# The first layer's hand-written list of steps in another order

## The chip, the cores and the metric

The kernel runs on one core of a Trainium2 chip. The time is that of one execution on the device, in microseconds (us), from start to end; the median of three runs is given. A core has five engines that run side by side, each through its own queue and in order: TensorE (PE, matrix products; its weight loads are shown as PEld), VectorE (DVE), ScalarE (ACT), GpSimd (POOL) and SyncE (SP, here a queue for transfers). They wait for each other by semaphores.

## The reference

A graph network of three layers over 2500 nodes with 256 features and 80000 edges sorted by destination. Cut to what matters:

```python
def _edge_conv(x, src, dst, W, b):
    xi = x[dst]; xj = x[src]
    m = jnp.concatenate([xi, xj - xi], axis=-1) @ W + b
    s = jax.ops.segment_sum(m, dst, num_segments=N)
    cnt = jax.ops.segment_sum(jnp.ones((dst.shape[0],), m.dtype), dst, num_segments=N)
    return s / jnp.maximum(cnt, 1.0)[:, None]

h = jnp.maximum(_layernorm(x, axis=-1), 0.0)
xs = [h]
for W, b in ((W0, b0), (W1, b1), (W2, b2)):
    h = jax.nn.relu(_edge_conv(h, src, dst, W, b)); xs.append(h)
out = x + jnp.concatenate(xs, axis=-1) @ Wf + bf
```

## The kernel before

**Tiles.** The nodes are 20 tiles of 128, taken in ten pairs q = 0 to 9. The sum over the edges is a product with a matrix of counts, `a`: how many edges go from node m to node n. It is built on the chip from the list of edges and used by all three layers. A window is six destinations; 417 windows stand in five groups of up to 84, and a step of counting takes four windows at a time (b = 0 to 104; 0 to 20 are the first group).

**Staging.** Layer 0 has two hand-written lists of step names, `order` (line 906) and `later` (line 1151). The program goes through both, one name after the other, and each name issues its instructions (table `acts`, from line 889, and `steps`, from line 1141). An engine keeps the order in which its instructions were issued; across engines only data and free buffers count. So the list sets the order within each engine's queue and nothing else. Layers 1 and 2 and the end follow by loops that the change leaves alone.

**The steps of `order`, by what they do** (the number behind a name is the pair, the part of the edges, or the counting step):

- Start: `dstr` (ACT) copies the destinations; `lim`, `first`, `pi` (`find_rows`, DVE), `next`, `pk` (`pick_half`, PE), `sg` (`count_half`, ACT), `se` (`search`, DVE), `pb` (PE) and `sa` (DVE) search where each of four parts of the edges begins. `io` (`small_numbers`, ACT) makes three small tables. `ge` (`get_edges`, POOL) gathers the edges of a part by two indirect DMAs.
- Layer norm: `st` (`stats`, DVE, a pair of tiles), `sq` (ACT), `sc` and `of` (DVE), for the groups of pairs 0, 1, 2 to 3, 4 to 7 and 8 to 9. Then the pair's two tiles are normalized: `N` on POOL twice, `Nd` on DVE twice, `Nm` on DVE and ACT, `Np` on POOL and ACT (`normalize`, line 751).
- Products: `T` (`turn`, PE) turns a pair, `R` (`take_turned`, ACT) copies it out, `Z` and `F` (`product`, PE) multiply it by the layer's and the last weights; `H` (ACT) and `L` (DVE) split Z's result in a high and a low part, `V` (DVE) adds a bias, `G` (ACT) takes F's.
- Keys of a part of the edges: `aw` (ACT); `kr` (`find_room`), `kw`, `ka` (`key_parts`), `kb` (`key_high`) and `kc` (`key_node`) on DVE; `km` (ACT); `kt` (`key_turn`, PE); `k1` and `k2` (`key_copy`, ACT). In the profile these write `room`, `away`, `lo_i`, `es` or `hi_i`, `kn`, `km`, and `key_m` and `key_n`.
- Counting: `B` (`compare`, line 825, DVE) compares keys with a row of numbers, for two counting steps at once, by one instruction for `one_m` and two for `one_n`; a `B` whose step was done already does nothing. `C` (`counts`, PE) multiplies them; `E` (`take_counts`, ACT) copies the counts to `a`.
- `warm` stores how many matmuls without use the next product, turn or pick on PE issues first:

```python
def keep_warm(n):
    cold[0] = n
```

**Buffers.** `one_m` and `one_n` have three buffers each (`AT_ONCE`), and two PSUM banks of one pool serve `pk`, `pb`, `kt` and `C` up to the first `g`.

**The steps of `later`:** `g` begins a group's sum, `u` is one tile of it (four matmuls), `o` its own term, `r` its end; `c` is a turn of up to four counting steps for the next group on PE, `e` takes one, `b` compares two; `d` finds degrees; `f` writes a finished group to memory; `x` adds the input by a DMA on POOL's queue; the rest prepare weights and the next layer.

**Loads.** The transfers of the input and the first weights are issued ahead of both lists (lines 414 to 457): x in five chunks, `own_w` (the second half of the layer's weights, needed by `Z`), the last weights (needed by `F`), and the first half.

Of the kernel before, what the change touches and what calls it, by code (L numbers as in the profile page):

```python
# [298 lines left out]
def by_windows(ctx: ExitStack, tc: tile.TileContext, x, src, dst, Ws, bs, Wf, bf, out, missing):  # L299
# [130 lines left out]
    ws = [None] * L  # L430
# [88 lines left out]
    first = pp.tile([P, 1], F32, name="first")  # L519
# [358 lines left out]
    def by_count(g):  # L878
# [25 lines left out]
        "warm": keep_warm,  # L904
    }
    order = """
        warm7 dstr lim first st0 sq0 io next pi0 sc0 of0 Nm0 pi1 st1 pk00 sg00 se00 st2 warm4 pk01 sg01 se02 T0
        R0 sq1 sc1 se01 of1 pk10 pk30 se04 se03 sg30 sg10 Z0 st4 pk20 Np1 pk21 sg21 T1 st5 st6 F0 sg20 pk11 st7
        se10 ge0 R1 st3 pb0 sa0 G0 sq3 sc3 F1 st9 aw0 kr0 ka0 H0 se11 kb0 sg11 pk31 kw0 Nd7 sg31 Z1 N6 T6 se12
        kc0 se14 km0 sq2 sc2 G1 T7 se13 st8 R6 ge1 kt0 k10 pb1 of3 sa1 sq4 Nm5 sc4 R7 L0 k20 of4 Nm9 H1 Z6 F6 T9  # L910
        B0 B1 aw1 kr1 T5 G6 of2 F7 R5 R9 C0 ge2 aw2 G7 C1 E0 E1 Z9 Np8 B2 B3 B5 V9 C2 E2 C3 T8 H6 B4 kw1 ka1 kb1
        ge3 Z5 L1 kc1 E3 C5 km1 kr2 aw3 H5 ka2 kb2 kr3 L5 kt1 k11 kw3 k21 ka3 N2 T2 R2 kw2 Z7 C6 kb3 C4 kc2 Z2
        E5 R8 B7 kc3 C7 B6 Nm3 km3 C8 E4 km2 T3 E6 N4 T4 kt2 L6 E7 E8 B9 H9 L9 kt3 k13 Z8 C10 k22 k23 k12 C9 R3
        Z3 H2 B8 B11 B12 H7 L7 E10 E9 C12 E12 B13 C11 E11 L2 H3 F3 G3 C14 E14 C13 F5 B10 B15 C16 C15 R4 Z4 B17
        E13 E15 E16 C17 C18 G5 F4 B19 C19 H8 L8 E17 E18 H4 C20 F2 G4 E20 E19 B16 B18
        """

    second = ctx.enter_context(ExitStack())
# [56 lines left out]
    E12 = 4096.0  # L975
    C1 = 1.0 + 1.0 / E12
# [160 lines left out]
    def take_next(it=iter(range(len([b for b in windows if b[0] == 0]), len(windows)))):  # L1137
# [11 lines left out]
        "h": each((late_final, (q,)) for q in LATE),  # L1149
    }  # L1150
    later = """
        g d u u d u u L3 B23 ws w B21 d d u u c B24 B14 G2 L4 d d e B22 B20 u u u e e e b b b c e d u e e d d d
        f u u b b u c u b u e e d y u e e x b c o o o e e e b c e x b b b e e e u o e u e d d c e u u r d d g u
        w u u b w c e u d e e d d d b u b w u u e c b e e e e u f u c u e u u x u u b b b e e c e d d d u u y p
        e e o e e o b c u p o e b d d e d e u u e d d c b b b e u d y p o r g u u c e e u u b b u u u u d e e c
        e o o b u y e e e c b b e e u u e u e u c p o u u u e o b b c b b b u e e e f u u e e d e e c p e u r g
        u u c e d d u f b b u u u u c u u d e e e u o e e b b c b o e e e e e b p u u u u c e e b b d b b u e e
        u b c u e u u k e e e d d e c e y o s u o r f s s v g v v u u u s u u u u u p v q u l u o u u u q o u u
        u u u n n n p o n l q q h h o u u r x
        """  # L1160
    acts.update(steps)
    for name in (order + later).split():
# [269 lines left out]
    for l in range(1, L):  # L1432
# [7 lines left out]
        for i in range(Q + LAG):  # L1440
            if 0 < i <= Q:
                lone.make(i - 1)
            if i < Q:
                q = order[i]
                n = Nodes(l, q)
# [53 lines left out]
    for i, q in enumerate(order):  # L1499
# [9 lines left out]
        for k in range(2):  # L1509
            t = 2 * q + k  # L1510
            add_to_acc(t, po[k])
            n = P if t < NT - 1 else LAST
            if i < Q - 4 and q < Q - 1:
                if k:
                    d = SPo.dma_start(out[(t - 1) * P:(t + 1) * P, :].rearrange("(k p) d -> p k d", p=P),
                                      acc[:, t - 1:t + 1, :])
            else:
                d = (ACTo if i >= Q - 4 and k else SPo).dma_start(out[t * P:t * P + n, :], acc[:n, t, :])
# [11 lines left out]
def gnn_kernel(tc: tile.TileContext, x, src, dst, Ws, bs, Wf, bf, out):  # L1530
    nc = tc.nc
    with tc.tile_pool(name="flag", bufs=1) as flag:
        missing = flag.tile([1, 1], I32, name="missing")
        tc.mark_branch_hint_location("again", "LikelyTaken",
                                     engines=[getattr(mybir.EngineType, e) for e in ("PE", "DVE", "Activation")])
        near_end = by_windows(tc, x, src, dst, Ws, bs, Wf, bf, out, missing)
        loads, (again,) = nc.values_load_multi_w_load_instructions(missing, min_val=0, max_val=1)

        for d in loads:
            if d.ins.engine in [getattr(mybir.EngineType, e) for e in ("PE", "DVE", "Activation")]:  # L1540
                tc.add_manual_dep(d.ins, near_end.ins.name,
                                  mybir.DependencyInfo(mybir.DependencyClass.Sync, mybir.DependencyReason.DATA),
                                  reason="behind the outputs")
        with tc.If(again > 0, label="again"):
            general(tc, x, src, dst, Ws, bs, Wf, bf, out)
# [28 lines left out]
```

## Time and profile before

| | us |
|---|---|
| median of three runs | 460.54 (460.31 to 460.66) |
| the profiled execution | 459.55 |
| its span, from the first to the last instruction | 457.6 |

The profile is of one execution. Its page gives the busy time of each engine and, in 40 slices of 11.4 us, the busy share in tenths. A row of the timeline has the start (us from the span's start), the duration, the engine, the operation, what it writes and reads, and in brackets how long the engine had been idle before it and what ended that. Several equal instructions in a row are one row (x2). The durations of rows on one engine overlap a little, since an instruction begins before the one ahead has quite ended; so the distance from start to start is what it costs in a queue. A row of the windows has, after the stretch and its length, the busy us (and the instructions) of PE, PEld, DVE, ACT and POOL, then the granted clock of PE as a share of full speed, the share of the DMA engines and GB/s.

### The profile page before, as it was taken

The numbers are of one execution on the slowest core, as the hardware profiler recorded it, in microseconds if no ns is written. First come the engines' busy times: TensorE is split into PE (matmuls) and PEld (weight loads), VectorE is DVE, ScalarE is ACT, GpSimd is POOL, SyncE is SP. The second block draws the span as 40 slices with busy tenths as digits, with TensorE's granted clock in tenths as the row PEclk, the third lists the DMA queues.
The fourth block names the chain that finished last, engine by engine and source line by source line (L and its number), as shares of the span: only waits on it lengthen the run. The fifth ranks groups of instructions, "written<-read, shape, count | busy, mean of one in ns | idle before, by whom it ended". The sixth has DMA issues, their size and how long they took to land.

```text
span 457.6 us, 7441 instructions
## 1 busy us (share of the span) xinstructions
PE 447.6 (98%) x2733; PEld 358.2 (78%) x2733; DVE 375.2 (82%) x724; ACT 319.7 (70%) x586; POOL 41.2 (9%) x64
## 2 busy tenths in 40 slices
PE   6999999999999999999999999999999999999995
PEld 3887887788888878878878868867888787688685
DVE  7999989899998755299979859876999687569795
ACT  6888877785757553587879849756877897597540
POOL 4690103111001010100000000000000000000000
PEclk9999999999999999999999999999999999999999
DMA  8310179882629276341396522011124855220015
GB/s 279 101 47 1 24 149 151 171 136 51 122 58 183 51 184 141 98 93 45 115 362 227 181 91 92 0 45 47 46 56 146 319 185 178 90 92 1 1 62 166
DMA packets 22056, 52.47 MB, mean 115 GB/s; under 512 B 1931, under 2 KB 12382, under 8 KB 22014
## 3 DMA queue, kind: packets, MB, share of 16 engines
q1 hardware_dynamic: 14654, 33.83, 22.3%
q0 software_dynamic: 5856, 16.48, 18.9%
q10 hardware_dynamic: 1504, 1.63, 1.0%
q8 instruction: 22, 0.36, 0.3%
q14 instruction: 20, 0.16, 0.1%
HBM read 36.47 MB, written 15.62 MB: 114 GB/s over the span
## 4 chain that ended last, share of the span: by engine, by line
PE 92%; DVE 4%; DMA 2%; issue 0%; ACT 0%; SPq 0%
PE bank L267 92%; DMA own_w<-in_L_gnn_W_dram 2%; DVE one_m L267 1%; DVE one_n L267 1%; DVE acc L267 0%; DVE lo_i L267 0%; DVE room L267 0%; DVE st L267 0%; DVE zl L267 0%; SPq L267 0%; DVE away L267 0%; DVE kn L267 0%; DVE es L267 0%; ACT away L267 0%; ACT acc L267 0%
## 5 line engine op out<-in xcount | busy, mean ns | idle before, releaser
L267 ACT CAST block<-staged 128x1008 fp32r<-128x1008 bf16 x120 | 118.0, 1031 | 16.7 <-DVE staged L267 6.4
L267 PE MATMUL bank<-block,zh 128*128 128x504 f32 (+1 forms) x200 | 83.7, 418 | 0.0
L267 PE MATMUL bank<-a,zh 128*128 128x504 f32 (+1 forms) x200 | 80.3, 401 | 0.0
L267 PE MATMUL bank<-a,zl 128*128 128x504 f32 (+1 forms) x200 | 77.9, 389 | 0.0
L267 PE MATMUL bank<-block,zl 128*128 128x504 f32 (+1 forms) x200 | 77.2, 386 | 0.0
L267 ACT CAST a<-bank 128x480 fp32r<-128x480 f32 (+1 forms) x105 | 52.8, 566 | 25.3 <-PE bank L267 25.0
L267 PE MATMUL bank<-block,sh 128*128 128x504 f32 x160 | 69.1, 432 | 0.0
L267 DVE TENSOR_TENSOR one_m<-iota_m,key_m 128x2048 bf16<-128x2048 bf16 (+2 forms) x55 | 64.2, 1166 | 6.0 <-PE bank L267 6.0
L267 PE MATMUL bank<-block,sl 128*128 128x504 f32 x160 | 62.5, 390 | 0.0
L267 PE MATMUL bank<-block,staged 128*128 128x512 f32 (+1 forms) x288 | 62.4, 368 | 0.0
L267 PEld LDWEIGHTS bank<-block,staged 128*128 128x128 f32 x288 | 49.4, 188 | 9.9 <-issue 0.7
L267 DVE TENSOR_TENSOR block<-staged 128x1008 fp32r<-128x1008 bf16 x40 | 47.0, 1205 | 5.3 <-PE bank L267 3.9
L267 PEld LDWEIGHTS bank<-block,zh 128*128 128x128 f32 x200 | 37.6, 188 | 10.8 <-issue 2.3
L267 PEld LDWEIGHTS bank<-block,zl 128*128 128x128 f32 x200 | 37.6, 188 | 10.6 <-issue 3.2
L267 PEld LDWEIGHTS bank<-a,zl 128*128 128x128 f32 x200 | 37.7, 188 | 7.0 <-issue 0.2
L267 PEld LDWEIGHTS bank<-a,zh 128*128 128x128 f32 x200 | 37.6, 188 | 7.0 <-issue 0.2
L267 DVE TENSOR_TENSOR one_n<-iota_n,key_n 128x640 bf16<-128x640 bf16 (+2 forms) x110 | 42.5, 428 | 0.0
L267 PEld LDWEIGHTS bank<-block,sh 128*128 128x128 f32 x160 | 30.1, 188 | 10.5 <-issue 3.5
L267 PEld LDWEIGHTS bank<-block,sl 128*128 128x128 f32 x160 | 30.1, 188 | 9.3 <-issue 3.7
L267 DVE TENSOR_TENSOR staged<-staged 128x1008 bf16<-128x1008 bf16 x40 | 27.2, 679 | 12.0 <-ACT block L267 11.6
L267 PEld LDWEIGHTS <-one_m 128*128 128x128 bf16 x834 | 29.2, 98 | 9.0 <-issue 3.5
L267 PE MATMUL bank<-own_w,hT 128*128 128x256 f32 x144 | 34.8, 386 | 0.7 <-DMA own_w<-in_L_gnn_W_dram 0.7
(192 smaller groups left out, 641.7 us busy)
## 6 DMA issues: line engine op xcount, KB each, us to landing
staged<-a_dram SPq DMA_DIRECT2D x52, 504.0 KB
a_dram<-a POOLq DMA_DIRECT2D x20, 630.0 KB, 8.8
acc<-in_x_dram POOLq DMA_DIRECT2D x3, 640.0 KB, 8.8
out_dram<-acc SPq DMA_DIRECT2D x5, 256.0 KB
acc<-in_x_dram SPq DMA_DIRECT2D x2, 512.0 KB
acc<-in_x_dram ACTq DMA_DIRECT2D x1, 768.0 KB
out_dram<-acc SPq DMA_DIRECT2D x5, 128.0 KB
wt<-in_L_gnn_W_dram SPq DMA_DIRECT2D x2, 256.0 KB
```

Of the source, the lines that this page charges most:

```text
L267: return self.tc.keep_in_program_order(call(*args, **kwargs))
```

## The change

The two lists get another order. All names appear as often as before; nine names that stood in `later` (B14, B20 to B24, G2, L3 and L4) now stand in `order`'s text, ahead of the first `g`. No function changes.

```diff
--- before.py
+++ after.py
@@ -904,15 +904,16 @@
         "warm": keep_warm,
     }
     order = """
-        warm7 dstr lim first st0 sq0 io next pi0 sc0 of0 Nm0 pi1 st1 pk00 sg00 se00 st2 warm4 pk01 sg01 se02 T0
-        R0 sq1 sc1 se01 of1 pk10 pk30 se04 se03 sg30 sg10 Z0 st4 pk20 Np1 pk21 sg21 T1 st5 st6 F0 sg20 pk11 st7
-        se10 ge0 R1 st3 pb0 sa0 G0 sq3 sc3 F1 st9 aw0 kr0 ka0 H0 se11 kb0 sg11 pk31 kw0 Nd7 sg31 Z1 N6 T6 se12
-        kc0 se14 km0 sq2 sc2 G1 T7 se13 st8 R6 ge1 kt0 k10 pb1 of3 sa1 sq4 Nm5 sc4 R7 L0 k20 of4 Nm9 H1 Z6 F6 T9
-        B0 B1 aw1 kr1 T5 G6 of2 F7 R5 R9 C0 ge2 aw2 G7 C1 E0 E1 Z9 Np8 B2 B3 B5 V9 C2 E2 C3 T8 H6 B4 kw1 ka1 kb1
-        ge3 Z5 L1 kc1 E3 C5 km1 kr2 aw3 H5 ka2 kb2 kr3 L5 kt1 k11 kw3 k21 ka3 N2 T2 R2 kw2 Z7 C6 kb3 C4 kc2 Z2
-        E5 R8 B7 kc3 C7 B6 Nm3 km3 C8 E4 km2 T3 E6 N4 T4 kt2 L6 E7 E8 B9 H9 L9 kt3 k13 Z8 C10 k22 k23 k12 C9 R3
-        Z3 H2 B8 B11 B12 H7 L7 E10 E9 C12 E12 B13 C11 E11 L2 H3 F3 G3 C14 E14 C13 F5 B10 B15 C16 C15 R4 Z4 B17
-        E13 E15 E16 C17 C18 G5 F4 B19 C19 H8 L8 E17 E18 H4 C20 F2 G4 E20 E19 B16 B18
+        io dstr warm4 lim first st0 sq0 warm7 next pi0 pk00 sg00 sc0 pi1 of0 Nm0 pk01 sg01 st1 sq1 se00 T0 R0
+        pk10 st2 pk20 sg20 sg10 sc1 se02 se01 of1 se04 se03 Np1 ge0 Z0 H0 st5 st7 pk30 sg30 pb0 sa0 T1 R1 st6
+        st4 sq3 F0 se10 pk31 se11 sg31 sc3 aw0 st3 sq2 pk11 sg11 N6 F1 pk21 sg21 st9 G1 Z1 Nd7 se12 G0 se13 of3
+        se14 T6 kr0 ge1 R6 H1 st8 sq4 pb1 kw0 ka0 T7 R7 kb0 L0 sc2 F6 kc0 km0 kt0 sa1 k10 k20 sc4 of4 Nm9 F7 Nm5
+        ge3 B0 B1 T9 ge2 aw1 kr1 R9 T5 ka1 Np8 Z6 C0 N2 kb1 N4 kw1 R5 C1 G7 of2 H6 B2 B3 Z9 L6 V9 B5 B4 kc1 Nm3
+        E0 E1 T8 aw2 aw3 C3 R8 C2 Z5 E2 L1 T2 G6 C5 B7 B6 C4 E3 km1 kr2 R2 Z7 E5 H5 kr3 C6 E4 ka2 ka3 H9 kt1 k11
+        Z2 k21 kw3 kb3 km2 C7 kb2 E6 C8 kw2 L5 km3 kc3 kc2 T3 E7 E8 T4 R4 B9 kt3 k23 k13 kt2 k22 B8 Z8 k12 L9
+        C10 R3 C9 Z3 H7 B11 C12 H2 C11 F3 E10 E9 L7 E12 E11 B12 B13 B10 C14 C13 L2 H8 F5 E14 E13 B15 C15 C16 Z4
+        G3 G5 B17 B19 C18 C17 F4 L8 E15 E16 C20 B16 B18 H4 E17 H3 B23 B21 B24 L4 B14 E18 C19 F2 E20 E19 G4 B22
+        B20 L3 G2
         """
 
     second = ctx.enter_context(ExitStack())
@@ -1149,14 +1150,14 @@
         "h": each((late_final, (q,)) for q in LATE),
     }
     later = """
-        g d u u d u u L3 B23 ws w B21 d d u u c B24 B14 G2 L4 d d e B22 B20 u u u e e e b b b c e d u e e d d d
-        f u u b b u c u b u e e d y u e e x b c o o o e e e b c e x b b b e e e u o e u e d d c e u u r d d g u
-        w u u b w c e u d e e d d d b u b w u u e c b e e e e u f u c u e u u x u u b b b e e c e d d d u u y p
-        e e o e e o b c u p o e b d d e d e u u e d d c b b b e u d y p o r g u u c e e u u b b u u u u d e e c
-        e o o b u y e e e c b b e e u u e u e u c p o u u u e o b b c b b b u e e e f u u e e d e e c p e u r g
-        u u c e d d u f b b u u u u c u u d e e e u o e e b b c b o e e e e e b p u u u u c e e b b d b b u e e
-        u b c u e u u k e e e d d e c e y o s u o r f s s v g v v u u u s u u u u u p v q u l u o u u u q o u u
-        u u u n n n p o n l q q h h o u u r x
+        g ws x u u d c d e b b b e u u u d u u u e e d d d c u e e e d d e d d u d b u c b d y e e b u d u u o o
+        c e u u e e e u b b c b b b f u c e u e e o o e d e e d e d u r w g c b u u b b e e e d d w y e w u u c
+        u u u u e b c d e e w b b e p e e e b u u u c b b o e d e o e e e u u u d d p d d d c f e u u b b u u u
+        e e e d d y c d u o o e f r g c u u u e e b b p u u e e c e e b b b u o o c b e e u u b d u u u c p o e
+        u u b e c o y e e e e d u u u e e e u e b b p d d e c e e f b b u u u r c g u e e u e e b c e e u e e u
+        u b x b c b u u b e u b c o e e e u e e e e u o d b c d p u u u e e e b b c d d y e x u u u o b e k v o
+        v u u v v p s f u u r g u o q p u o u u u u u l n n u u q u n u s u n o s o q h q u u u u l h u u u u x
+        s r
         """
     acts.update(steps)
     for name in (order + later).split():
```

## The prediction

> **What bounds the kernel now.** I read the page first: the span, the shares of the engines and the slices.
>
> ```profile
> span 457.6 us, 7441 instructions
> ...
> PE 447.6 (98%) x2733; PEld 358.2 (78%) x2733; DVE 375.2 (82%) x724; ACT 319.7 (70%) x586; POOL 41.2 (9%) x64
> ...
> PE   6999999999999999999999999999999999999995
> ```
>
> PE is busy in every slice but the first and the last. The change moves work and takes no useful work away, so the time can fall only where PE now stands idle or waits. Next I read the chain that ended last, in order of time, for where PE is not its carrier.
>
> ```profile
> 1.74 7.93 DMA own_w<-in_L_gnn_W_dram
> ...
> 9.81 4.44 PE bank L267 x22
> ...
> 14.27 0.59 ACT acc L267
> ...
> 35.38 1.22 DVE one_m L267
> 36.59 0.73 DVE one_n L267 x2
> ...
> 37.37 415.48 PE bank L267 x2524
> ```
>
> Three stretches can be seen. Up to 9.81 us the start hangs on a DMA, the first weights. From 14.27 to 37.37 us the chain runs almost wholly over DVE. From 37.37 us PE carries it to the end, 415.48 us without a break. Whatever the change wins, it wins before 37.37 us, and it keeps it only if PE isn't made to wait behind that point.
>
> How long PE waits in the middle stretch stands in the rows of the weight loads, whose gaps are real (the ends of matmuls are modelled):
>
> ```profile
> 31.55 0.11 PEld L267 LDWEIGHTS <-kn 128*128 128x128 bf16 x2 [0.70 <-DVE kn L267]
> ...
> 34.37 1.59 PEld L267 LDWEIGHTS bank<-own_w,hT 128*128 128x128 f32 x8
> 37.37 0.56 PEld L267 LDWEIGHTS <-one_m 128*128 128x128 bf16 x16 [1.41 <-DVE one_n L267]
> ```
>
> The wait of 0.70 us is for the keys of one part of the edges (kc1 ahead of kt1), that of 1.41 us for the comparison B7 ahead of C7. Together 2.11 us: more than that this change cannot win behind 9.81 us.
>
> **The change part by part.**
>
> *The start.* The rows show what PE does before the first product Z0.
>
> ```profile
> 4.49 0.71 ACT L267 CAST dst_r<-dst_i 128x625 fp32r<-128x625 int32 x1 [1.23 <-DMA dst_i<-in_dst_dram]
> ...
> 5.95 0.28 ACT L267 CAST iota_m<-im_i 128x128 bf16<-128x128 int32 x1
> ...
> 6.77 1.04 PE L267 MATMUL bank<-idle 128*128 128x512 bf16 x4
> ...
> 8.56 0.59 ACT L267 ACTIVATE hT<-bank 128x512 f32<-128x512 f32 x1
> ```
>
> "io" (three casts, from 5.95 us) moves into ACT's wait of 1.23 us for the edges, so ACT is free some 0.7 us sooner at 6 us. On DVE "pi1" (start to start 6.91 to 7.90 us, 0.99 us) moves ahead of of0 and Nm0. So the first tile's turn T0 (7.65 us now) cannot come sooner: about 8.0 to 8.4. Its copy R0 also stands behind sq1, which needs st1 (DVE, to about 8.9); I get R0 at 9.1 to 9.7 where the row has 8.56 to 9.15. Z0 needs own_w, landed at 9.67 us, so all of this is covered: Z0 stays at 9.8. Without that cover it would cost 0.5 us. The start is worth 0, within 0.1 us either way.
>
> One thing goes that the words of the change don't mention. "warm4" now stands ahead of "warm7", and keep_warm only stores a number: the 4 is overwritten, and the row with four idle matmuls (1.04 us, ahead of pk01) goes away. PE was waiting there anyway; worth 0, or a rival below.
>
> *Up to B0.* Between Z0 and C0 PE gets the same matmuls in both lists (8 picks but those ahead of Z0, Z0 F0 F1 Z1 F6 Z6 F7, five turns, one key turn), and DVE the same instructions up to B0. The tiles N6 on POOL need sc3, which needs st4 to st7 and sq3; sq3 no longer stands behind G0, so N6 starts near 14.7 in place of 15.39, and ends at 17.2. The keys of part 0 now follow it. What this saves is the difference to instructions of the same form and size that ran apart from POOL:
>
> ```profile
> 15.39 2.46 POOL L267 TENSOR_SCALAR acc<-acc,mv,rs 128x256 f32<-128x256 f32 x2 [1.50 <-DVE rs L267]
> ...
> 16.04 0.32 DVE L267 SCALAR_TENSOR_TENSOR room<-iota_m,lead,away 128x128 bf16<-128x128 bf16 x1
> ...
> 16.27 0.49 DVE L267 TENSOR_SCALAR lo_i<-es 128x256 int32<-128x256 int32 x1
> ...
> 16.80 0.53 DVE L267 TENSOR_SCALAR es<-es 128x256 int32<-128x256 int32 x1
> ...
> 34.24 0.28 DVE L267 SCALAR_TENSOR_TENSOR away<-room,away 128x128 bf16<-128x128 bf16 x1
> ...
> 34.44 0.28 DVE L267 TENSOR_SCALAR lo_i<-es 128x256 int32<-128x256 int32 x1
> ...
> 34.84 0.28 DVE L267 TENSOR_SCALAR hi_i<-es 128x256 int32<-128x256 int32 x1
> ```
>
> 0.04 + 0.21 + 0.25 = 0.50 us. It is given back: kt0, which was turned at 18.79 us, now stands behind F6 on PE. F6 starts after Z1, T6, pb1 and T7 (about 19.1) and takes 1.6 us, so kt0 comes at 20.8, the copies k10 and k20 at 21.2 and 21.7, and B0 at about 21.7, where it starts at 21.37 now. se12 also waits for the last count sg21, which now stands behind aw0 on ACT: some 0.5 us of DVE. So DVE is 0.25 us *late* at B0 (between 0.3 early and 0.8 late), and PE, by the same count, about 0.25 us late at C0 (R6 ahead of F6).
>
> *B0 to B9.* Here is the gain. These rows show the keys of parts 1 to 3 beside POOL's N2 and N4, and a comparison beside Np8:
>
> ```profile
> 22.41 1.21 DVE L267 TENSOR_TENSOR one_m<-iota_m,key_m 128x2048 bf16<-128x2048 bf16 x1
> ...
> 24.26 0.56 DVE L267 SCALAR_TENSOR_TENSOR room<-iota_m,lead,away 128x128 bf16<-128x128 bf16 x1
> 24.48 1.36 POOL L267 TENSOR_SCALAR acc<-acc,mv,rs 128x256 f32<-128x256 f32 x1
> ...
> 24.82 1.42 DVE L267 TENSOR_TENSOR one_m<-iota_m,key_m 128x2048 bf16<-128x2048 bf16 x1
> ...
> 28.96 3.97 POOL L267 TENSOR_SCALAR acc<-acc,mv,rs 128x256 f32<-128x256 f32 x3
> ...
> 29.27 0.70 DVE L267 TENSOR_SCALAR lo_i<-es 128x256 int32<-128x256 int32 x1
> ...
> 30.01 0.53 DVE L267 TENSOR_SCALAR es<-es 128x256 int32<-128x256 int32 x1
> ...
> 30.46 0.68 DVE L267 TENSOR_TENSOR zl<-bank,zh 128x512 fp32r<-128x512 f32 x1
> ...
> 31.42 0.59 DVE L267 SCALAR_TENSOR_TENSOR room<-iota_m,lead,away 128x128 bf16<-128x128 bf16 x1
> ...
> 31.93 0.72 DVE L267 TENSOR_SCALAR lo_i<-es 128x256 int32<-128x256 int32 x1
> ...
> 32.69 0.55 DVE L267 TENSOR_SCALAR es<-es 128x256 int32<-128x256 int32 x1
> ...
> 33.16 0.56 DVE L267 SCALAR_TENSOR_TENSOR room<-iota_m,lead,away 128x128 bf16<-128x128 bf16 x1
> ```
>
> Against 0.28 each: rooms 0.28 + 0.31 + 0.28, low parts 0.42 + 0.44, high parts 0.25 + 0.27, together 2.25 us. In the new list kr1 ka1 kb1 kw1 stand straight behind B1, at about 24.7 to 25.5, while POOL still issues the gathers ge1, ge3, ge2 (se13 lets it begin near 18 in place of 19.27; 2.6 to 3 us each by now's starts, so to about 26), and the parts 2 and 3 stand behind B7, at about 34, when N4 is over (26 + 1.36 + 2.6 + 2.6 = 32.6). All 2.25 us should go.
>
> In their place the comparisons B3, B5 and B7 run beside Np8, N2 and N4. Beside Np8 a one_m took 1.42 in place of 1.21 us, 0.21 more; B3 bears that now too, so 0.42 us is added for B5 and B7. For the one_n no row stands beside a tile; I take 0, the lower end is 0 and the upper that of a low part, 0.44 us for each of six. zl is not slowed (0.68 beside POOL at 30.46 us, and 0.68 at 42.87 us, quoted below, where POOL rests), so L6, V9 and L1 cost the same there.
>
> The gathers and tiles on POOL are due before T8 (27.8), T2 (30.4) and T4 (37): with Np8 at 27.4, N2 at 30.0 and N4 at 32.6 they come in time, Np8 and N2 by only 0.4 us.
>
> Sum for DVE at B9 and behind it: 2.25 − 0.42 − 0.25 = 1.58 us sooner. The wait of 1.41 us goes, because B7 stands ahead of eight key instructions (about 34 in place of 37.3), and the 0.70 us too, because kt1 moved behind C6. PE alone could gain 2.11 − 0.25 = 1.86 us. What is late next is DVE again:
>
> ```profile
> 40.00:50.00 10.00, 10.00 (x101) 8.73 (x100) 10.00 (x19) 8.20 (x18) 0.00 (x0) 1.00 0.01 2
> ```
>
> ```profile
> 42.87 0.68 DVE L267 TENSOR_TENSOR zl<-bank,zh 128x512 fp32r<-128x512 f32 x1
> ...
> 47.06 0.80 DVE L267 TENSOR_TENSOR one_n<-iota_n,key_n 128x640 bf16<-128x640 bf16 x2
> ...
> 47.94 0.76 PEld L267 LDWEIGHTS <-one_m 128*128 128x128 bf16 x16
> ```
>
> DVE has no gap in 40 to 50 us, and B15 ends at 47.86, 0.08 us before C15 and C16 need it. PE can thus gain at most 1.58 + 0.08, say 1.65 us there; behind it DVE runs ahead. I take off 0.3 us for ACT: by my count of its queue k12 and R3 end at about 39.9, just when Z3 could start, and its banks (E6 before C8, k13 before C10) come within 0.3 us of their need. **1.35 us** remain.
>
> *The second list.* The first turn of counts stands behind two units of the sum in place of six. By now's rows (0.23 us a matmul, four a unit) PE comes to it 3.6 us sooner, but B21 moved ahead too: I count it done 0.7 us before. Later turns lag DVE by at most as much as this one, so I cost the list at 0, up to 0.7 us lost.
>
> **The rivals.**
>
> A. *ACT takes over.* For it: ACT is busy 8.90 and 8.20 of 10 us in the two stretches, and in the new order its queue has little left. Each 0.1 us of delay in R3 or E6 passes to PE. Half of the gain is left: 0.3 to 0.9 us, time 459.9.
>
> B. *The clock falls.* Without warm4 PE has little to do between 5.4 and 9.8 us. At the end of the run the granted clock shows what idleness does:
>
> ```profile
> 456.00:457.60 1.60, 0.00 (x0) 0.00 (x0) 0.00 (x0) 0.00 (x0) 0.00 (x0) 0.53 0.06 15
> ```
>
> The last matmul ends at about 452.85, and a mean of 0.53 over 1.6 us is full speed for 0.1 and half for the rest: after some 3.2 us. In the new start no gap is longer than about 1.4 us, which speaks against it. If it fell near 9 us, Z0 and F0 would run at half speed for about as long, 3.2 us, and PE would lose up to 1.6: time 460.7. [...]
>
> C. *The comparisons suffer as the keys did* (slower). Place: B3, B5, B7, nine instructions beside five tiles on POOL. If each were longer by a low part's 0.42 us, DVE would lose 3.8 − 0.21 us, save 2.25, be late by 0.25, and come 1.6 us later than now; with 0.08 us to spare at C15 PE stands 1.5 us longer: time 462.0. It decides from a mean of 0.25 us for each of the nine ((2.25 − 0.25 + 0.21)/9). Against it: one_m lost only 0.21. At the far end each of the five tiles would hold DVE for its whole length: 1.36 + 2.6 + 2.6 − 0.21 = 6.35 us lost, DVE 4.35 and PE 4.3 us late, 464.8; but the keys met three and a half tiles and lost 2.25 us in all, so I give this 0.02 of C's chance. [...]
>
> D. *The second list stalls* at the first turns of counts and gives the gain back: 460.5.
>
> **How the numbers follow.** Forecast (1 to 1.9 us gained) 0.47; A 0.22; B 0.10; C 0.14; D 0.07. The profiled execution took 459.55 us (span 457.6 and 1.95 around it), 0.99 under the median of the runs; the gain is worked out inside its span and taken off the median: 460.54 − 1.35 = 459.2, and a span of 456.25. The range takes in A, B and D and leaves out the far part of C: 458.5 (all 2.0 us of PE's waits) to 461.3. A measurement of this kernel can tell about 0.2%, 0.92 us, from no change: faster by more takes most of the forecast and little of A, 0.50; within, 0.36; slower, 0.14.
>
> **What would show it.** Right: the gaps of 0.70 and 1.41 us are gone, lo_i and room at 0.28 to 0.3, Z3 (41.70 now) near 40.2, and PE without a break from there. Wrong: one_m or one_n beside tiles well over 1.42 and 0.5; B0 later than 22.2; Z0 to F1 at more than 0.2 us a matmul (clock); a wait of PE on ACT at C8, C9 or Z3; or a gap ahead of the first 32 counts.

## The result, and the profile after

The changed kernel is slower: 462.56 us, median of 15 runs (461.37 to 465.05), against 460.54 us, median of 15 runs of the kernel before beside it (459.15 to 461.72). The ratio, taken over all these runs (that of the two medians alone is 1.0044), is 1.0051 with a 95% interval of 1.0034 to 1.0068. The forecast was 459.2 us with a range of 458.5 to 461.3. The profiled execution took 461.59 us. Its page, span and shares:

```profile
span 459.5 us, 7436 instructions
...
PE 448.4 (98%) x2729; PEld 358.7 (78%) x2729; DVE 374.4 (81%) x724; ACT 319.0 (69%) x586; POOL 42.2 (9%) x64
...
PE   6989999999999999999999999999999999999995
```

The four idle matmuls of the kernel before are gone (2729 in place of 2733), and PE is as full as it was. The chain that ended last, in order of time:

```profile
9.70 9.81 PE bank L267 x46
...
20.18 7.07 PE bank L267 x51
...
27.28 0.60 ACT hT L267
27.87 0.48 ACT acc L267
28.36 0.49 ACT hT L267
28.84 0.48 ACT acc L267
...
29.37 425.32 PE bank L267 x2608
454.69 0.03 issue
```

DVE no longer carries the stretch up to 37 us, as the prediction wanted. In its place stand four instructions of ACT between 27.28 and 29.33 us, and PE runs without a break only from there. The timeline of PE's weight loads, the waits in brackets:

```profile
9.70 2.58 PEld L267 LDWEIGHTS bank<-own_w,hT 128*128 128x128 f32 x8 [0.56 <-ACT hT L267]
...
20.18 1.59 PEld L267 LDWEIGHTS bank<-own_w,hT 128*128 128x128 f32 x8 [0.31 <-ACT hT L267]
...
29.37 1.59 PEld L267 LDWEIGHTS bank<-own_w,hT 128*128 128x128 f32 x8 [2.21 <-ACT acc L267]
47.32 0.56 PEld L267 LDWEIGHTS <-one_m 128*128 128x128 bf16 x16 [0.24 <-DVE one_n L267]
```

The waits of 0.70 and 1.41 us of the kernel before are gone. New are 0.31 us at F6, 2.21 us at Z9, and a quarter of a microsecond here and there on DVE. Z0's eight loads took 2.58 us in place of 1.59. Windows of the changed kernel (the sixth figure behind the comma is the granted clock), then of the kernel before:

```profile
8.00:10.00 2.00, 1.82 (x7) 1.33 (x8) 1.97 (x13) 1.90 (x7) 0.09 (x1) 0.58 1.10 352
10.00:12.00 2.00, 2.00 (x6) 1.61 (x6) 2.00 (x12) 1.37 (x7) 1.80 (x2) 0.57 1.10 347
```

```profile
8.00:10.00 2.00, 1.14 (x7) 0.72 (x6) 2.00 (x13) 1.95 (x8) 0.00 (x0) 1.00 1.10 360
10.00:12.00 2.00, 2.00 (x11) 1.79 (x11) 2.00 (x12) 1.03 (x4) 1.80 (x2) 1.00 1.10 349
```

In this execution the clock was down while Z0 ran, at 0.50 from 8.32 to 11.73 us; in that of the kernel before it was 1.00 there.

What does Z9 wait for? Z9 reads what R9 writes, and R9 (hT on ACT) reads the turn T9. ACT's timeline, then PE's, of the changed kernel:

```profile
24.29 0.68 ACT L267 ACTIVATE away<-ed,below 128x128 bf16<-128x128 int32 x2
27.28 0.60 ACT L267 ACTIVATE hT<-bank 128x512 f32<-128x512 f32 x1 [2.31 <-PE bank L267]
```

```profile
24.02 1.04 PE L267 MATMUL bank<-shift,acc 128*128 128x128 f32 x8
24.89 1.89 PE L267 MATMUL bank<-own_w,hT 128*128 128x256 f32 x8
26.62 0.67 PE L267 MATMUL bank<-one_n,one_m 128*128 128x60 bf16 x16
```

The eight turns of T9 and T5 were through the array by 25.06 us, yet ACT was released at 27.25 us, together with the end of the counts C0 and C1 (27.29). PE's rows were not late; what stands late in the trace are the semaphore events behind them, the events that the waits of other engines are read from. Those of T9, T5, Z6, C0 and C1 all stand between 27.25 and 27.59 us, T9's 2.64 us behind the end of its row (24.61), while nearly all others of the execution stand within 0.06 us of the end of their matmul. Beside it stands POOL. Its queue in the changed kernel, then in the kernel before:

```profile
18.71 1.16 POOL L267 DMA_INDIRECT ed<-in_dst_dram,start_i  x1 [0.68 <-DVE ends L267]
20.18 0.96 POOL L267 DMA_INDIRECT es<-in_src_dram,start_i  x1 [0.30 <-issue]
21.43 0.95 POOL L267 DMA_INDIRECT ed<-dst_e,start_i  x1 [0.30 <-DVE rs L267]
...
25.25 1.23 POOL L267 DMA_INDIRECT es<-in_src_dram,start_i  x1 [0.31 <-issue]
26.52 8.31 POOL L267 TENSOR_SCALAR acc<-acc,mv,rs 128x256 f32<-128x256 f32 x5
```

```profile
19.27 1.04 POOL L267 DMA_INDIRECT ed<-in_dst_dram,start_i  x1 [1.41 <-DVE start_i L267]
...
23.18 1.26 POOL L267 DMA_INDIRECT es<-in_src_dram,start_i  x1 [0.30 <-issue]
24.48 1.36 POOL L267 TENSOR_SCALAR acc<-acc,mv,rs 128x256 f32<-128x256 f32 x1
26.01 1.13 POOL L267 DMA_INDIRECT ed<-dst_e,start_i  x1 [0.17 <-issue]
```

The new list has all six gather issues (ge1 ge3 ge2) in a row and then five tiles in a row; the old one has four issues, a tile, two issues and the other tiles. Last, DVE's timeline of the changed kernel:

```profile
24.04 1.21 DVE L267 TENSOR_TENSOR one_m<-iota_m,key_m 128x2048 bf16<-128x2048 bf16 x1
...
25.90 0.69 DVE L267 SCALAR_TENSOR_TENSOR room<-iota_m,lead,away 128x128 bf16<-128x128 bf16 x1
26.51 0.28 DVE L267 TENSOR_SCALAR lo_i<-es 128x256 int32<-128x256 int32 x1
26.83 1.21 DVE L267 TENSOR_SCALAR es<-es 128x256 int32<-128x256 int32 x1
...
28.23 1.70 DVE L267 TENSOR_TENSOR one_m<-iota_m,key_m 128x2048 bf16<-128x2048 bf16 x1
...
31.75 1.44 DVE L267 TENSOR_TENSOR one_m<-iota_m,key_m 128x2048 bf16<-128x2048 bf16 x1
```

The keys of part 1 fell on POOL's last gather issue and first tile: 0.69 + 0.28 + 1.21 us, where three of that form take 0.84 apart from POOL.

To compare runs apart from the clock at the start, I use one measure below, **the stretch**: from the end of Z0's weight loads to the end of the chain's last PE row. Here 29.37 + 425.32 − (9.70 + 2.58) = 442.41 us; in the kernel before 37.37 + 415.48 − (9.78 + 1.59) = 441.48. So 0.93 us of the loss lies in the stretch and 0.91 in the later end of Z0's loads (12.28 against 11.37).

### The profile page after: what moved, and what is told of

It reads as the page before. It is cut to its first block, busy times and chain, and to the rows that moved or that the text cites. A ratio compares the mean times of both kernels' runs of the same rounds, so it can differ in the third digit from the quotient of the medians.

```text
span 459.5 us, 7436 instructions
## 1 busy us (share of the span) xinstructions
PE 448.4 (98%) x2729; PEld 358.7 (78%) x2729; DVE 374.4 (81%) x724; ACT 319.0 (69%) x586; POOL 42.2 (9%) x64
## 4 chain that ended last, share of the span: by engine, by line
PE 96%; DVE 1%; DMA 1%; ACT 1%; issue 0%
PE bank L267 96%; DMA acc<-in_x_dram 1%; ACT hT L267 0%; DVE st L267 0%; DVE pick L267 0%; ACT acc L267 0%; DVE acc L267 0%; DVE behind L267 0%; DVE mv L267 0%; ACT rs L267 0%; DVE rs L267 0%; DVE off L267 0%; DVE after L267 0%
## 5 line engine op out<-in xcount | busy, mean ns | idle before, releaser
L267 PE MATMUL bank<-own_w,hT 128*128 128x256 f32 x144 | 36.1, 395 | 2.3 <-ACT acc L267 2.1
```

What stands on the lines that cost most here:

```text
L267: return self.tc.keep_in_program_order(call(*args, **kwargs))
```

## The experiments

Beside each run stands the kernel before on the same chip (460.62 to 460.85 us). "Hold-up" is ACT's wait for PE at R9 (in e3 at R5), "Z9" the pause in PE's weight loads ahead of Z9. The ratio is not that of the medians. The diffs show only the names around the edit.

| run | time, us (runs) | ratio, 95% interval | hold-up | Z9 | Z0's loads end | stretch |
|---|---|---|---|---|---|---|
| before, profiled | | | none | none | 11.37 | 441.48 |
| after, profiled | | | 2.31 | 2.21 | 12.28 | 442.41 |
| e1_warm_back | 462.42 (12) | 1.0039, 1.0021 to 1.0056 | 2.34 | 2.25 | 12.18 | 442.45 |
| e2_before_no_warm4 | 461.01 (12) | 1.0008, 0.9994 to 1.0023 | none | none | 12.92 | 441.57 |
| e3_order_alone | 461.47 (12) | 1.0022, 1.0007 to 1.0037 | 1.34 | 1.25 | 12.97 | 442.37 |
| e4_after_again | 461.70 (1) | | 2.36 | 2.28 | 12.77 | 442.38 |
| e5_counts_behind_z9 | 465.39 (1) | | 2.46 | 3.16 | 13.05 | 445.62 |
| e6_tile8_between_gathers | 460.70 (10) | 1.0011, 0.9997 to 1.0026 | none | none | 13.42 | 442.06 |
| e7_short_idle | 462.75 (7) | 1.0058, 1.0033 to 1.0083 | 2.42 | 2.33 | 13.30 | 442.37 |
| e8_second_list_alone | 461.73 (12) | 1.0017, 1.0006 to 1.0029 | none | none | 13.41 | 441.77 |
| e9_pool_as_before | 461.55 (12) | 1.0009, 0.9992 to 1.0025 | none | none | 12.68 | 441.28 |
| e10_gathers_swapped | 462.12 (1) | | 2.44 | 2.36 | 12.80 | 442.42 |
| e11_first_list_best | 460.89 (12) | 1.0000, 0.9983 to 1.0016 | none | none | 13.28 | 441.34 |
| e12_best_with_four | 460.24 (12) | 0.9991, 0.9978 to 1.0004 | none | none | 12.38 | 441.02 |

**e1: the four idle matmuls back in the changed kernel.**

```diff
-        io dstr warm4 lim first st0 sq0 warm7 next pi0 pk00 sg00 sc0 pi1 of0 Nm0 pk01 sg01
+        io dstr lim first st0 sq0 warm7 next pi0 pk00 sg00 sc0 pi1 of0 Nm0 warm4 pk01 sg01
```

> The changed list with warm4 set straight ahead of pk01 again, so that four idle matmuls run there as before. Theory 'clock': the granted clock stays at 1.00 up to 12 us (0.58 in the changed kernel), Z0's eight weight loads take 1.6 us in place of 2.58, PE's following steps come 1.0 us sooner, and the time falls by 1.0 us or more, to 461.5 or less. Theory 'order': the clock has little to do with it; the wait of PE of 2.2 us for ACT near 27 to 29 us stays, and the time stays above 462.

1.0039 against 1.0051, well inside each other's interval. Hold-up and stall stay to 0.04 us. The four are not the cause of the loss.

**e2: the kernel before without them.**

```diff
-        warm7 dstr lim first st0 sq0 io next pi0 sc0 of0 Nm0 pi1 st1 pk00 sg00 se00 st2 warm4 pk01
+        warm7 dstr lim first st0 sq0 io next pi0 sc0 of0 Nm0 pi1 st1 pk00 sg00 se00 st2 pk01
```

> The kernel before without its four idle matmuls ahead of pk01; nothing else changes. Theory 'clock': the clock falls to about half for some 3.4 us between 8 and 12 us here too, and the kernel is 0.7 to 1.5 us slower than before. Theory 'order': it stays within 0.3 us, since PE waits there anyway.

A difference of 0.08%, 0.4 us, that the interval doesn't tell from none. Its profile has Z0's loads at 3.05 us, near twice the 1.59, and no hold-up: the old order, too, meets the slow clock at the start. (The windows of this profile show a clock of 1.00 there, because its clock record begins only at 12.87 us; the length of the loads tells.)

**e3: the changed first list without the nine names, with the second list of before.**

```diff
-        G3 G5 B17 B19 C18 C17 F4 L8 E15 E16 C20 B16 B18 H4 E17 H3 B23 B21 B24 L4 B14 E18 C19 F2 E20 E19 G4 B22
-        B20 L3 G2
+        G3 G5 B17 B19 C18 C17 F4 L8 E15 E16 C20 B16 B18 H4 E17 H3 E18 C19 F2 E20 E19 G4
```

> The changed first list (without the nine names that moved into it) and the second list of before. Theory 'clock' and theory 'order' both put the loss before the second list: same time as the changed kernel, 462.5, and the same late start of the group sums (56.5 us against 54.9). Rival 'second list': the time comes back to 461 or less.

The stretch is that of the changed kernel (442.37 against 442.41), so the first list alone makes its loss. The pieces differ: R9 is on time at 26.29, R5 waits 1.34 us, the stall at Z9 is 1.25 us, and PE waits 0.57 us more at 35.12 us for a tile of POOL, whose five took 10.65 us. The time isn't that of the changed kernel: 1.0022 against 1.0051, between what the two sides expected (more on this at e8).

**e4: the changed kernel once more**, for a second profile.

> The changed kernel once more, for a second profile. If the wait of ACT for PE of 2.3 us ahead of the copy of the last pair's turn (27.3 us), and PE's 2.2 us behind it, come from the order, they stand in this profile too, at the same instructions within 0.3 us; if they were a chance delay of that one execution, they stand elsewhere or are gone, and PE's stalls behind 12 us sum to something else.

Hold-up and stall again, 2.36 and 2.28 us. They are no accident of one execution: they are in every profile that has the new order with POOL's six issues in a row (after, e1, e3, e4, e5, e7, e10), and in none without.

**e5: is it the end of PE's own work that lets the word go?** C0 and C1 behind Z9 on PE:

```diff
-        ge3 B0 B1 T9 ge2 aw1 kr1 R9 T5 ka1 Np8 Z6 C0 N2 kb1 N4 kw1 R5 C1 G7 of2 H6 B2 B3 Z9 L6
+        ge3 B0 B1 T9 ge2 aw1 kr1 R9 T5 ka1 Np8 Z6 N2 kb1 N4 kw1 R5 G7 of2 H6 B2 B3 Z9 C0 C1 L6
```

> The changed kernel with the counts C0 and C1 behind Z9 on PE. In the changed kernel R9 (hT on ACT) starts at 27.28 us, 2.31 us after ACT was free, though the turn T9 that it reads ended on PE near 24.6 us; the same moment is the end of C1 (27.29) and 0.8 us behind the end of the last gather on POOL (26.48). Theory P (PE tells of finished work late, when its run of work ends): PE's run now ends with Z6, so R9 starts near 26.8 and Z9 stalls 1.7 us in place of 2.21. Theory G (the gather beside it holds the message up): R9 stays at 27.3 and Z9 at 29.4. Theory F (PE's 16 KB instruction packet, which DMA queue 8 brings at 24.1 us in the middle of the gathers' traffic, holds it up): as G, 27.3.

The whole runs 1.1 us later than in the changed kernel, so the places are compared by what stands beside them. PE's timeline has Z6 over at 27.93; the last gather issue ends at 26.39 + 1.24 = 27.63; ACT's timeline shows R9:

```profile
28.59 0.60 ACT L267 ACTIVATE hT<-bank 128x512 f32<-128x512 f32 x1 [2.46 <-PE bank L267]
```

That is 0.66 us behind the end of PE's work and 0.96 behind the gather; in the changed kernel it was 0.80 behind the gather. Theory P falls; G stands, and so does F, which expected the same here. The time was a surprise: 465.39 us. Windows:

```profile
29.00:31.00 2.00, 0.32 (x1) 0.32 (x2) 2.00 (x4) 2.00 (x6) 2.00 (x3) 0.95 0.00 0
31.00:33.00 2.00, 2.00 (x6) 1.55 (x6) 1.40 (x4) 0.62 (x2) 2.00 (x2) 0.50 0.00 0
33.00:35.00 2.00, 2.00 (x23) 1.55 (x22) 0.60 (x2) 0.35 (x1) 2.00 (x2) 0.69 0.00 0
```

With the counts gone from in front of it, no weight load ran on PE for 3.16 us ahead of Z9 (2.75 us from the last matmul to the next), and then the clock was halved from 30.81 to 34.22 us. Z9's eight loads took 2.97 us in place of 1.59. Here the stall is paid twice: once as idle time, once as slow work behind it. The low clock lasted 3.41 us, as long as that at the start of the changed kernel (8.32 to 11.73).

**e6: a tile among the gathers.**

```diff
-        ge3 B0 B1 T9 ge2 aw1 kr1 R9 T5 ka1 Np8 Z6 C0 N2
+        ge3 B0 B1 T9 Np8 ge2 aw1 kr1 R9 T5 ka1 Z6 C0 N2
```

> The changed kernel with POOL's tile Np8 between the gathers ge3 and ge2; ge2 then runs from about 25.4 to 28.0 us in place of 23.9 to 26.5. Theory G: what is held up moves with ge2 and ends near 28.8, so R9 is on time (25.0) but a later one (R5, or the copies of the counts) is late by up to 2 us. Theory F: PE's instruction packet at 24.1 us stands beside no gather; R9 on time, no wait of ACT on PE over 0.5 us between 24 and 30 us, the stall of 2.21 us ahead of Z9 gone, 1 to 2 us sooner: 460.6 to 461.6. Theory P: R9 stays late at 27.2. The keys of part 1 then stand beside Np8 and ge2 in place of tiles only: room and es nearer 0.5 than 0.69 and 1.21.

One name moved on POOL: the wait at R9 and the stall at Z9 are gone, and the ratio falls from 1.0051 to 1.0011. That is also what theory F (PE's packet) expected; e7 tests it. A smaller delay is left: the keys' turn kt0 is released late (ACT waits 1.51 us for it where it waits 0.86 in e9), and the stretch, 442.06, is still 0.6 above the kernel before.

**e7: PE's instruction packet.** In the middle of the gathers, at 24.1 us, a packet of instructions arrives (16 KB on queue 8); I took it for PE's own. To move it, 28 short idle matmuls stand for 7 long ones:

```diff
-        for _ in range(cold[0]):
-            PEo.matmul(to, idle[:, :P], idle, start=True, stop=True)
+        for _ in range(4 * cold[0]):
+            PEo.matmul(to[:, :8], idle[:, :P], idle[:, :8], start=True, stop=True)
```

> The changed kernel with 28 idle matmuls of 8 columns in place of 7 of 512 at the start (the values that they make are never read). 21 more weight loads and matmuls put PE's instruction packet about 3 us sooner, near 21 us; the order of everything else stays. Theory F: the hold-up goes or falls where nothing waits for it, R9 starts near 25, Z9 without the 2.21 us: 460.5 to 461.2. Theories G and P: R9 at 27.3 and Z9 at 29.4 as before the edit: 462.3 to 462.8. All this up to what 21 short matmuls do to the start (0.3 us).

With 21 more loads and 21 more matmuls on PE the packet moved to 20.8 us, and hold-up and stall stayed (2.42 and 2.33). Theory F falls. The times lie in two groups: four runs from 462.14 to 462.75 at a mean clock of 0.999 to 1.0, three from 464.36 to 465.13 at 0.994 to 0.995. The changed kernel has three such runs too (464.31, 464.39 and 465.05, all at 0.994). Each fits a stall of 2.2 us with the halved clock of e5 behind it, but none of these runs was profiled, so that is argued, not shown; a low mean clock alone doesn't tell it either, since three runs of e11 at 0.992 took 460.88 to 461.31 us.

**e8: the second list alone**, the old first list with the nine names at its end.

```diff
-        E13 E15 E16 C17 C18 G5 F4 B19 C19 H8 L8 E17 E18 H4 C20 F2 G4 E20 E19 B16 B18
+        E13 E15 E16 C17 C18 G5 F4 B19 C19 H8 L8 E17 B23 B21 B24 B14 E18 H4 L4 C20 F2 G4 E20 E19 B16 B18 B22
+        B20 L3 G2
...
     later = """
-        g d u u d u u L3 B23 ws w B21 d d u u c B24 B14 G2 L4 d d e B22 B20 u u u e e e b b b c e d u e e d d d
+        g ws x u u d c d e b b b e u u u d u u u e e d d d c u e e e d d e d d u d b u c b d y e e b u d u u o o
...
```

> The kernel before with the second list of the changed one, and the nine names of layer 0 that it needs for that at the end of the first list (B21 B23 B24 B14 behind E17, L4 behind H4, B22 B20 L3 G2 last). Theory 'the first 57 us decide' (the loss is made by R9's wait and the clock's phase): as before, 460.2 to 460.9. Rival D of the prediction (the second list stalls): 461.3 to 461.8, with a gap of PE or a longer stretch behind 57 us.

The time is what this run's expectation gave rival D (461.73); the profile doesn't say so: the stretch is 0.3 us over that of the kernel before, and no wait over 0.3 us is new behind 57 us. Under the new first list the stretch hardly moves (441.28 in e9 with the changed second list, 441.34 in e11 with the old one). The times say more: in all three pairs that differ in the second list alone, the changed one is slower, e8 by 0.17% than the kernel before, the changed kernel 1.0051 against e3's 1.0022, e9 1.0009 against e11's 1.0000. That is 0.4 to 1.3 us. Of the three only e8's is clear of noise by its interval. So rival D isn't refuted, and what costs this time stays open: no profile shows the place. (Z0's loads ended at 13.41 us in e8's profile, the clock at the start again.)

**e9: POOL's queue as before**, everything else as changed.

```diff
-        ge3 B0 B1 T9 ge2 aw1 kr1 R9 T5 ka1 Np8 Z6 C0 N2 kb1 N4 kw1 R5 C1
+        ge2 Np8 ge3 N2 N4 B0 B1 T9 aw1 kr1 R9 T5 ka1 Z6 C0 kb1 kw1 R5 C1
```

> The changed kernel with POOL's queue as in the kernel before: ge1 ge2 Np8 ge3 N2 N4, so four gather issues, a tile, two issues, three tiles. I compare by the stretch from the end of Z0's weight loads to the end of PE's last matmul, which the phase of the clock at the start leaves out: 441.47 in before, 442.41 in the changed kernel, 442.04 with Np8 between ge3 and ge2. Theory G (six gather issues in a row hold up PE's messages; they go once the row is broken up): ACT waits for PE less than 0.5 us at R9, no stall of PE at Z9, the stretch 441.5 to 441.9, times 460.6 to 461.3, and no run above 463.0, since without the stall of 2.2 us the clock isn't taken down behind it. Rival (the order of PE, ACT and DVE makes the wait, whatever POOL does): R9 late by 1 to 2.3 us as now, 462.3.

POOL, ACT and PE's loads, a view each:

```profile
23.09 0.95 POOL L267 DMA_INDIRECT es<-in_src_dram,start_i  x1 [0.30 <-issue]
24.07 1.84 POOL L267 TENSOR_SCALAR acc<-acc,mv,rs 128x256 f32<-128x256 f32 x1
26.08 1.12 POOL L267 DMA_INDIRECT ed<-dst_e,start_i  x1 [0.17 <-issue]
```

```profile
25.77 1.07 ACT L267 ACTIVATE hT<-bank 128x512 f32<-128x512 f32 x2
```

```profile
30.38 0.56 PEld L267 LDWEIGHTS <-one_m 128*128 128x128 bf16 x16 [0.69 <-DVE one_n L267]
```

R9 and R5 run one behind the other without a wait, and Z9 comes with no stall. The first wait of PE behind F6 is 0.69 us on DVE. The stretch falls by 1.13 us, to less than that of the kernel before, and no run is above 462.2. The median, 461.55, is 0.25 above what was expected, the ratio 1.0009.

Not every event of PE is on time here. In e6, e9, e11 and e12 alike, that of F7 comes 0.36 to 0.41 us late, 0.9 us behind POOL's fourth issue, and that of C1 0.9 to 1.2 us late, 0.4 to 0.5 us behind the sixth; in e6 that of kt0 is late too, by 0.66 us. Only kt0's copy loses time by it. The kernel before, whose queue on POOL is that of e9, has no late event in this stretch. So the row of six makes the hold-up long and puts it in front of R9 and Z9; that events are late at all seems to take something else of the new order as well.

**e10: six issues in a row, in another order.**

```diff
-        kc0 km0 kt0 sa1 k10 k20 sc4 of4 Nm9 F7 Nm5 ge3 B0 B1 T9 ge2 aw1
+        kc0 km0 kt0 sa1 k10 k20 sc4 of4 Nm9 F7 Nm5 ge2 ge3 B0 B1 T9 aw1
```

> The changed kernel with ge2 ahead of ge3: still six gather issues in a row, in the order ge1 ge2 ge3, then the tiles. Theory G: the hold-up stays where it is in time, about from the fifth issue to 0.8 us behind the sixth: R9 near 27.3, the stall ahead of Z9 2.0 to 2.4 us. Rival (it belongs to the pair ge2, not to the row): it comes about 2.5 us sooner, between 21.5 and 24.8, where R7's and F6's neighbours wait, and R9 is on time.

```profile
27.94 0.60 ACT L267 ACTIVATE hT<-bank 128x512 f32<-128x512 f32 x1 [2.44 <-PE bank L267]
```

The hold-up stays in its place (ACT's timeline), 0.9 us behind the sixth issue, whichever pair that is.

**e11 and e12: what is left, at its best.** e9's POOL queue with the second list of before (e11), and that with the four idle matmuls back ahead of pk01 (e12).

> As the run with POOL's queue as before, and the second list of the kernel before too (the nine names back in it). What is left of the change is the order of PE, ACT and DVE in layer 0. If the changed second list costs 0.25 us (441.76 against 441.5 in the run of the second list alone) and the row of gathers all the rest, the stretch from Z0's loads to the last matmul is 441.2 to 441.7 and the time 460.1 to 460.9, as before. If the gain of 1.35 us that the prediction saw between B0 and B9 is there and only covered: 440.1 to 440.5, and 459.2 to 459.6. If the new order itself costs: 442.0 or more, over 461.2.

> The last run (POOL's queue and the second list as before) with the four idle matmuls back ahead of pk01, so that PE's start has the same idle work as the kernel before. If the four matter (rival B: without them more runs go through Z0 at half clock; the kernel before without them took 1.0008 of its time, 0.9994 to 1.0023): the shortest runs come down by about 0.5 us, median 460.2 to 460.6, the mean clock of most runs 0.998 to 1.0 in place of 0.992 to 0.999. If not: 460.7 to 461.1, as without them. In both cases the stretch from Z0's loads to the last matmul is 441.2 to 441.4, and no version of the new order beats the kernel before by more than 0.5 us.

e11 is the kernel before in time, 1.0000. e12 has the shortest stretch of all, and 0.9991 (0.9978 to 1.0004): a version that may beat the kernel before by a tenth of a per cent, which this measurement can't tell from nothing. The mean clock of its runs is 0.994 to 1.0, that of e11's 0.992 to 0.999. That the four matter by 0.4 us is likely from this and from e2, and not shown. The stretch, too, moves by 0.3 us between these two, which differ in the start alone, so less than that can't be read from it.

## Why the prediction was wrong

**The start** held in place but not in length. Z0 began at 9.70 us (9.8 forecast); what it waited for last was R0 (9.1 to 9.7 forecast; hT on ACT, to 9.65 us), no longer its weights. But its loads took 2.58 us, with the clock at 0.50 up to 11.73 us, though between 1.7 and 8.3 us no pause in PE's weight loads was over 1.35 us; the 3.2 us without work ahead of the fall at the end of the run were no bound. That is what rival B described (whose time, 459.2 + 1.6, should read 460.8), and the four missing matmuls are at most part of its cause: with them Z0's loads took 1.59 us in the kernel before and in e12, but 2.26 in e1 and 2.44 in e8, so it differs from execution to execution. Without them all ten profiles have more, 2.58 to 3.06. In time the four are worth 0.4 to 0.6 us by three pairs (e1 and the changed kernel, e2 and the kernel before, e12 and e11), none of them clear of noise. The profile of before that I argued from was a lucky one, 0.99 us under its own median, and I took the edit off that median without asking what made the luck.

**Up to B0.** Part 0's keys ran clean as forecast (0.34, 0.28 and 0.29 us). B0 came at 23.00 us, not at 21.7. Of the 1.3 us, 0.9 are the end of Z0's loads. Counted from there, B0 is 0.72 us later than before (10.72 against 10.00) where 0.25 to 0.3 was forecast; 0.31 of it is F6, which waits for R6 (the row at 20.18).

**B0 to B9, DVE.** The 2.25 us for the keys of parts 1 to 3 came in only for parts 2 and 3, behind the last tile. POOL was on time (its tiles began at 26.52, forecast 26), but DVE was 1.2 us late, and part 1's keys, due at 24.7 to 25.5, ran from 25.90: 2.18 us in place of 0.84, and of the 1.79 of before. A saving of 0.95 became a loss of 0.39. The comparisons cost 0.28 + 0.23 us more at B3 and B5 and nothing at B7 (0.51 against 0.42 forecast). From B0 to B9 DVE takes 17.36 us (23.00 to 40.36) where it took 17.12 (21.37 to 38.49). In e9 it takes 16.16, in e11 15.79: there the gain is, 1.0 to 1.3 us of the 1.83 forecast, but B0 starts 10.7 and 11.4 us behind Z0's loads in place of 10.0, which takes most of it back in e9 and all of it in e11.

**B0 to B9, PE: the step that failed.** "I take off 0.3 us for ACT": I had gone through ACT's queue for what it has to do and for when its inputs are *computed*, at C8, C9 and Z3. At R9 the input was computed in time (T9 ended at 24.61 us), and ACT learned of it 2.6 us later and stood for 2.31. The 2.11 us of waits went as forecast, and 2.21 us at Z9 took their place. Rival A had the right engine and the wrong place and cause, and took off 0.45 to 1.05 us (it left 0.3 to 0.9 of the 1.35) where the stall was 2.2. What makes it so long is in the change, in an edit that I costed only by its due times: ge3 ahead of ge2 and Np8 on POOL, six issues in a row. Taking the row apart (e6, e9, e11, e12) takes the waits at R9 and Z9 away; reordering inside it (e10), PE's later work (e5) and PE's instruction packet (e7) don't. Since e9 moves the tiles off part 1's keys too, not all of its 1.13 us of stretch is the hold-up's; the two can't be told apart by these runs.

**Of the 2.0 us**, then, 0.93 lie in the stretch and go with POOL's queue (e9: −1.13). The rest lies outside it. Candidates are the clock at the start, runs in which the clock went down behind the stall (argued from the times of e7 and the profile of e5), and what the second list costs; how the rest divides among them is not shown.

**The second list** costs 0 to 0.3 us of stretch, near the 0 given, but 0.4 to 1.3 us by the three pairs of times, where I allowed up to 0.7. **Rival C** was right in part: one instruction (es, 1.21) nearly reached what I gave 0.02, while the comparisons stayed near the 0.21 of before (0.28 and 0.23 more). That its 462.0 lies near the measured 462.56 is chance: it had PE wait for DVE near C15, and PE waited for ACT at Z9.

## What to carry to other kernels

When instructions are reordered, look not only at when each result is ready but at when the engine that needs it is released, and at what stands beside that moment; the row to look for is an engine that waits for PE long after PE's row has ended. Where such a wait stands beside a long row of gather issues on GpSimd, try the row broken up by other work, as e6 and e9 did here (ACT's wait at R9 went from 2.31 us to none). And before an edit is costed against one profiled execution, find out what that execution was lucky in, here the clock at the first large product (1.00 against 0.58).

## What was not expected of the hardware

- In the changed kernel PE's semaphore events stood up to 2.6 us late in the trace (T9: matmul ends at 24.61, event at 27.25) while PE itself went on through Z6, C0 and C1. In the seven profiles with six gather issues in a row, the hold-up ends 0.8 to 0.96 us behind the sixth. With the row broken up shorter delays remain (at e9). Why the kernel before, with four issues in a row, has none stays open; so does what delays the events.
- A pause of 3.16 us in PE's weight loads (2.75 us between matmuls) was followed by a clock of 0.50 for 3.41 us (e5). In the profile of the changed kernel the pause of 2.21 us at Z9 was not: the clock stood at 1.00 from 27 us to the end of PE's work.
- POOL's tiles and DVE slowed each other where they met: five tiles took 8.31 us here and 6.64 (1.36 + 5.28 on POOL's timeline) in the kernel before, es 1.21 us in place of 0.28, a comparison 1.70 in place of 1.21. But lo_i, begun at 26.51 us, 0.01 ahead of the first tile, took its 0.28. And the comparison, which lost 0.49 us beside tiles of 1.66 on average (8.31 / 5), was not held for a whole one.
